# Layer 2's ternary 3x3 convolution in float32r, over the image's upper and lower parts, by half images

## The chip, the cores and the metric

The kernel runs on one core of one Trainium2 chip. Time is the device time of one execution in microseconds (us). Engines are named as the profile names them: PE is TensorE's matmul, PEld its weight load, DVE VectorE, ACT ScalarE, POOL GpSimd.

## The reference, cut to what matters

Four images of 256 channels and 48 x 48 pixels pass four layers, each with a group normalisation before it and a residual sum after it. Layer 2 is a 3x3 convolution with weights of -1, 0 and +1, scaled per output channel:

```python
delta = 0.7 * abs_w.mean(axis=(1, 2, 3), keepdims=True)
ternary = jnp.where(w > delta, 1.0, jnp.where(w < -delta, -1.0, 0.0))
alpha = (abs_w * mask).sum(axis=(1, 2, 3), keepdims=True) / count
...
x = x + conv3x3(_gn(x), alpha * ternary)        # padding 1, NCHW
```

Layer 0 is a 7x7 attention over dilated patches, layer 1 a 3x3 convolution of signs, layer 3 a windowed attention. Layers 0 to 2 go image by image, layer 3 follows for all images.

## The kernel before

An image lies in SBUF as two channel tiles of 128 partitions. Layer 2 normalises it into a padded copy, and each block of 8 output rows (384 columns of PSUM) is the sum of 2 x 9 matmuls:

```python
def conv3x3(pad, w_sb, evacuate):            # layers 1 and 2; the matmul is L457
    for mo in range(NCT):                    # 2 halves of the output channels
        for rb in range(NRB):                # 6 blocks of 8 rows
            ps = ps_cv.tile([P, RB, W], F32, tag="cv", name="cv3")
            n = 0
            for ct in range(NCT):
                for t in range(T1):
                    r0, c0 = rb * RB + t // 3, t % 3
                    nc.tensor.matmul(ps, w_sb[:, ct, t, mo * P : (mo + 1) * P],
                        pad[:, ct, r0 : r0 + RB, c0 : c0 + W],
                        start=(n == 0), stop=(n == NCT * T1 - 1))
                    n += 1
            evacuate(ps, mo, rb)

def layer2(xt, b):
    m, r = gn_stats(xt, ps_st)
    pad = padp.tile([P, NCT, H1, H1], F32, tag="pad", name=f"pad2_{b}")
    clear_border(pad, 1, H1)
    for ct in range(NCT):
        normalise(pad[:, ct, 1 : 1 + H, 1 : 1 + W], xt, ct, m, r)   # one VectorE instruction
    ...                                       # evacuate: xt += alpha * ps, on VectorE
    conv3x3(pad, wl2_sb, evacuate)
    ...                                       # store the image, statistics for layer 3
```

The pool of padded copies has two buffers. One holds the next image's input of layer 0's first convolution (conv0, L334), whose matmuls stand before and after layer 2 in TensorE's order. `prepare_layer2` makes the ternary weights once, beside conv0 of image 0: one load of all weights, absolute values, sums over TensorE, two comparisons. The scheduler decides the order of instructions on each engine.

Of the kernel before, what the change touches and what calls it, by code (L numbers as in the profile page):

```python
# [10 lines left out]
F32 = mybir.dt.float32  # L11
BF16 = mybir.dt.bfloat16
F32R = mybir.dt.float32r
AF = mybir.ActivationFunctionType
ALU = mybir.AluOpType
# [4 lines left out]
P = 128  # L20
B, C, H, W = 4, 256, 48, 48
HW = H * W
NCT = C // P

RB = 8
NRB = H // RB
# [17 lines left out]
T1 = 9  # L44
H1 = H + 2
# [49 lines left out]
def conv_preact_kernel(  # L95
# [22 lines left out]
    nc = tc.nc  # L118
# [51 lines left out]
    def normalise(dst, xt, ct, m, r):  # L170
        nc.vector.tensor_scalar(  # L171
            dst, xt[:, ct], m[:, ct : ct + 1], r[:, ct : ct + 1], ALU.subtract, ALU.mult
        )

    def clear_border(t, pad, n):
        nc.gpsimd.memset(t[:, :, 0:pad, :], 0.0)
        nc.gpsimd.memset(t[:, :, n - pad : n, :], 0.0)
        nc.gpsimd.memset(t[:, :, pad : n - pad, 0:pad], 0.0)
        nc.gpsimd.memset(t[:, :, pad : n - pad, n - pad : n], 0.0)


    with (
# [20 lines left out]
        for ki in range(K0):  # L203
            for ct in range(NCT):
                nc.scalar.dma_start(
                    out=w1_sb[:, ct, ki * K0 : (ki + 1) * K0, :],
                    in_=w1[ct * P : (ct + 1) * P, ki * K0 : (ki + 1) * K0, :],
# [15 lines left out]
        for z in band_d:  # L223
            for f in range(NPH):
                nc.sync.dma_start(
                    out=z[f, 0 : QB * ZROW].rearrange("(p s) -> p s", s=ZROW), in_=zero
# [14 lines left out]
        nc.vector.tensor_add(off, off, bn["be"])  # L241

        wl1_sb = wts.tile([P, NCT, T1, C], BF16, name="wl1_sb")
        wl2_sb = wts.tile([P, NCT, T1, C], F32, name="wl2_sb")
        alpha = wts.tile([P, NCT], F32, name="alpha")

        def prepare_layer1():
# [3 lines left out]

        def prepare_layer2():

            nc.sync.dma_start(out=wl2_sb, in_=wl2.rearrange("(ct p) t o -> p ct t o", p=P))
            tmp = padp.tile([P, 3, T1, C], F32, tag="pad", name="wl2_tmp")
            ab, hi, lo = tmp[:, 0], tmp[:, 1], tmp[:, 2]
            delta = smx.tile([P, 2, C], F32, tag="delta", name="delta", bufs=1)
            ps = ps_st.tile([P, C], F32, tag="st", name="abs_ps")
            for ct in range(NCT):
                nc.scalar.activation(ab, wl2_sb[:, ct], AF.Abs)  # L260
                for t in range(T1):
                    nc.tensor.matmul(
                        ps,
                        ones,
                        ab[:, t, :],
                        start=(ct == 0 and t == 0),
                        stop=(ct == NCT - 1 and t == T1 - 1),
                    )
            nc.vector.tensor_scalar(
                delta[:, 0, :], ps, 1.0 / (C * T1), 0.7, ALU.mult, ALU.mult  # L270
            )
            nc.vector.tensor_scalar_mul(delta[:, 1, :], delta[:, 0, :], -1.0)

            sums = smx.tile([P, NCT, NCT, 2], F32, tag="sums", name="sums", bufs=1)
            for ct in range(NCT):
                nc.scalar.activation(ab, wl2_sb[:, ct], AF.Abs)
                nc.vector.tensor_tensor(
                    hi, wl2_sb[:, ct], delta[:, 0:1, :].to_broadcast([P, T1, C]), ALU.is_gt
                )
                nc.vector.tensor_tensor(  # L280
                    lo, wl2_sb[:, ct], delta[:, 1:2, :].to_broadcast([P, T1, C]), ALU.is_lt
                )
                nc.vector.tensor_sub(wl2_sb[:, ct], hi, lo)
                nc.vector.tensor_add(hi, hi, lo)
                nc.vector.tensor_mul(ab, ab, hi)
                for what, src in ((0, ab), (1, hi)):
                    for mo in range(NCT):
                        ps = ps_st.tile([P, 1], F32, tag="st", name="sum_ps")
                        for t in range(T1):
                            nc.tensor.matmul(  # L290
                                ps,
                                src[:, t, mo * P : (mo + 1) * P],
                                ones[:, 0:1],
                                start=(t == 0),
                                stop=(t == T1 - 1),
                            )
                        nc.vector.tensor_copy(sums[:, ct, mo, what : what + 1], ps)
            nc.vector.tensor_add(sums[:, 0], sums[:, 0], sums[:, 1])
            nc.vector.tensor_scalar_max(sums[:, 0, :, 1], sums[:, 0, :, 1], 1.0)
            nc.vector.reciprocal(sums[:, 1, :, 1], sums[:, 0, :, 1])  # L300
            nc.vector.tensor_mul(alpha, sums[:, 0, :, 0], sums[:, 1, :, 1])
# [144 lines left out]
                    xs = by_phase(xt, mo)[:, py, :, k * RP : k * RP + nr, :]  # L446
                    nc.vector.tensor_add(xs, xs, pss[mo][:, py * DIL : (py + 1) * DIL])

        def conv3x3(pad, w_sb, evacuate):
            for mo in range(NCT):  # L450
                for rb in range(NRB):
                    ps = ps_cv.tile([P, RB, W], F32, tag="cv", name="cv3")
                    n = 0
                    for ct in range(NCT):
                        for t in range(T1):
                            r0, c0 = rb * RB + t // 3, t % 3
                            nc.tensor.matmul(  # L457
                                ps,
                                w_sb[:, ct, t, mo * P : (mo + 1) * P],
                                pad[:, ct, r0 : r0 + RB, c0 : c0 + W],  # L460
                                start=(n == 0),
                                stop=(n == NCT * T1 - 1),
                            )
                            n += 1
                    evacuate(ps, mo, rb)

        def layer1(xt, b):
            m, _ = gn_stats(xt, ps_st)
            neg = small.tile([P, NCT], F32, tag="neg", name="neg")
            nc.vector.tensor_scalar_mul(neg, m, -1.0)  # L470
            pad = padp.tile([P, NCT, H1, H1], BF16, tag="pad", name=f"pad1_{b}")
            clear_border(pad, 1, H1)

            for ct in range(NCT):
                nc.scalar.activation(
                    pad[:, ct, 1 : 1 + H, 1 : 1 + W], xt[:, ct], AF.Sign, bias=neg[:, ct : ct + 1]
                )

            def evacuate(ps, mo, rb):
                xs = xt[:, mo, rb * RB : (rb + 1) * RB, :]  # L480
                nc.vector.tensor_add(xs, ps, xs)

            conv3x3(pad, wl1_sb, evacuate)

        def layer2(xt, b):
            m, r = gn_stats(xt, ps_st)
            pad = padp.tile([P, NCT, H1, H1], F32, tag="pad", name=f"pad2_{b}")
            clear_border(pad, 1, H1)
            for ct in range(NCT):
                normalise(pad[:, ct, 1 : 1 + H, 1 : 1 + W], xt, ct, m, r)  # L490

            def evacuate(ps, mo, rb):
                xs = xt[:, mo, rb * RB : (rb + 1) * RB, :]
                nc.vector.scalar_tensor_tensor(  # L494
                    xs, ps, alpha[:, mo : mo + 1], xs, ALU.mult, ALU.add
                )

            conv3x3(pad, wl2_sb, evacuate)
            for ct in range(NCT):
                nc.sync.dma_start(out=x3_d[b][ct * P : (ct + 1) * P], in_=xt[:, ct])  # L500
            m, r = gn_stats(xt, ps_st)
            nc.vector.tensor_copy(st3[:, b, 0, :], m)
            nc.vector.tensor_copy(st3[:, b, 1, :], r)
# [20 lines left out]
        for b in range(B + 1):  # L524
            last = b - 1
            if b == B:
                attend0(last, NBLK - 1)
                finish0(last, NBLK - 2)
                finish0(last, NBLK - 1)
                layer1(xts[last], last)  # L530
                layer2(xts[last], last)
                break
# [462 lines left out]
```

## Time and profile before

| | before |
|---|---|
| time, median (range) | 5846.0 us (5844.4 to 5849.5, 4 runs) |
| span of the profiled run | 5851.2 us |
| TensorE busy | 95% of the span |
| layer-2 convolution on TensorE (float32) | 560.2 us in 4 images: 139.5 us in image 0, 141.7 in the last |
| layer-1 convolution (bfloat16, half as many records) | 147.6 us |
| granted TensorE clock, mean | 0.982 |

In a line of a group, the columns are: line of the kernel, engine, operation, output <- inputs, shape, count | total busy us, mean ns of one | idle time just before and what ended it. A timeline line has start and duration in us first. The lines that carry the reading stand in the prediction.

### The profile page before, as it was taken

The page shows a single profiled execution, that of the slowest core. Times are in us where ns is not written, and L with a number is a line of the kernel's source. Part 1 is how long each engine was busy: PE and PEld are TensorE (multiplying, and loading weights), DVE is VectorE, ACT ScalarE, POOL GpSimd, SP SyncE. Part 2 cuts the span into 40 slices and gives each one's busy share as a digit, 9 for nine tenths or more (in the row PEclk, how much of TensorE's full clock was granted, in tenths as well). Part 3 has the DMA queues.
Part 4 walks back from the last instruction along what each step waited for, and adds up shares of the span by engine and source line. Part 5 has one row for each costly group of instructions (what it writes and reads, how often), then busy time and mean ns, then how long its engine had stood idle before and what let it go on. Part 6 is the DMA issues. An engine that isn't in the chain of part 4 may idle for free.

```text
span 5851.2 us, 65381 instructions
## 1 busy us (share of the span) xinstructions
PE 5535.8 (95%) x25684; PEld 2763.7 (47%) x25684; DVE 2169.4 (37%) x5202; ACT 1075.7 (18%) x2179; POOL 732.0 (13%) x1193
## 2 busy tenths in 40 slices
PE   7999999999999999978999999999999999899997
PEld 3555555555555555544444444444444444444443
DVE  1210101110110110214566555565645665566654
ACT  0000000010000000013322223322223222233221
POOL 0000000000000000034202213112223012100111
PEclk9999999999999999889999999999999999999998
DMA  3000000000000001035122242132342222411322
GB/s 124 6 11 10 7 13 25 11 11 5 33 11 5 11 17 12 12 113 158 60 66 81 78 123 82 42 95 81 86 117 70 65 81 77 116 30 44 91 58 64
DMA packets 234350, 321.67 MB, mean 55 GB/s; under 512 B 94107, under 2 KB 199355, under 8 KB 227259
## 3 DMA queue, kind: packets, MB, share of 16 engines
q1 hardware_dynamic: 191995, 201.45, 12.9%
q0 software_dynamic: 38160, 108.02, 6.9%
q10 hardware_dynamic: 3888, 8.00, 0.4%
q8 instruction: 205, 3.36, 0.2%
q14 instruction: 102, 0.84, 0.0%
HBM read 209.43 MB, written 109.46 MB: 54 GB/s over the span
## 4 chain that ended last, share of the span: by engine, by line
PE 82%; DVE 6%; issue 4%; DMA 4%; POOL 3%; ACT 1%; SPq 0%; DVEq 0%; POOLq 0%; ACTq 0%
PE cv L334 27%; PE acc L817 25%; PE cv L457 12%; PE s L765 11%; DVE sm L807 4%; PE out_ps L879 3%; PE proj_ps L635 2%; PE ap L437 1%; DVE o L874 1%; POOL xn L621 1%; DMA nr<-n_d 1%; PE proj_ps L674 1%; DMA o_d<-stage 0%; POOL sq L683 0%; ACT sm L815 0%
## 5 line engine op out<-in xcount | busy, mean ns | idle before, releaser
L807 DVE TENSOR_TENSOR sm<-s,masks 128x240 f32<-128x240 f32 (+22 forms) x4032 | 1689.0, 456 | 1120.6 <-PE s L765 687.9
L817 PE MATMUL acc<-sm,vst 128*64 128x320 f32 (+14 forms) x13440 | 1985.9, 398 | 120.7 <-DVE sm L807 104.3
L334 PE MATMUL cv<-pad,w_sb 128*128 128x480 f32 (+1 forms) x3920 | 1575.4, 560 | 0.2 <-DVE pad L313 0.2
L817 PEld LDWEIGHTS acc<-sm,vst 128*64 128x64 f32 x13440 | 762.0, 136 | 851.6 <-issue 405.1
L334 PEld LDWEIGHTS cv<-pad,w_sb 128*128 128x128 f32 x3920 | 735.4, 189 | 785.8 <-issue 726.1
L815 ACT COPY sm<-s 128x528 f32<-128x528 f32 (+3 forms) x1440 | 690.7, 486 | 1601.9 <-DVE sm L807 1587.8
L765 PE MATMUL s<-qs,kst 128*128 128x320 f32 (+3 forms) x2880 | 838.6, 374 | 9.6 <-DVE sm L807 8.6
L765 PEld LDWEIGHTS s<-qs,kst 128*128 128x128 f32 x2880 | 436.1, 189 | 742.7 <-issue 694.8
L457 PE MATMUL cv<-pad,wl_sb 128*128 128x384 f32 (+1 forms) x2592 | 707.8, 436 | 4.6 <-DVE pad L171 3.2
L358 DVE TENSOR_TENSOR e<-lg,bn_inv 120x196 f32<-120x196 f32 (+1 forms) x20 | 7.2, 361 | 1171.9 <-PE lg L355 1171.9
L457 PEld LDWEIGHTS cv<-pad,wl_sb 128*128 128x128 f32 x1728 | 327.6, 190 | 233.7 <-issue 5.0
L343 ACT ACTIVATE k<-cv,b_sb 128x480 f32<-128x480 f32 (+1 forms) x20 | 12.9, 644 | 1606.5 <-PE cv L334 1606.5
L879 PE MATMUL out_ps<-o,wout_sb 128*128 128x384 f32 x576 | 222.5, 514 | 45.3 <-DVE o L874 44.4
L831 POOL DMA_DIRECT2D o_d<-stage x192 | 96.9, 505 | 1312.0 <-ACT sm L815 1055.9
L827 ACT COPY stage<-acc 128x384 f32<-128x384 f32 x288 | 137.8, 479 | 484.5 <-PE acc L817 479.6
L387 POOL COPY flat<-pad 128x240 f32<-128x240 f32 (+1 forms) x80 | 34.6, 460 | 1516.8 <-PE trx L400 1480.8
L494 DVE SCALAR_TENSOR_TENSOR x<-cv,alpha,x 128x384 f32<-128x384 f32 x48 | 29.7, 618 | 501.9 <-PE cv L457 501.9
L879 PEld LDWEIGHTS out_ps<-o,wout_sb 128*128 128x128 f32 x576 | 100.2, 191 | 139.5 <-DVE o L874 66.9
L437 PEld LDWEIGHTS ap<-seen,xT 120*128 120x128 f32 (+2 forms) x832 | 110.7, 212 | 16.1 <-ACT seen L430 10.1
L139 ACT ACTIVATE rsq_s<-gn_v 128x2 f32<-128x2 f32 x16 | 3.3, 204 | 622.2 <-DVE gn_v L166 622.1
L674 PE MATMUL proj_ps<-wv_sb,xn 128*128 128x256 f32 x288 | 96.6, 441 | 20.2 <-ACT sg L652 12.6
L457 PEld LDWEIGHTS <-wl_sb 128*128 128x128 bf16 x864 | 85.6, 99 | 62.6 <-issue 6.5
(118 smaller groups left out, 1978.3 us busy)
## 6 DMA issues: line engine op xcount, KB each, us to landing
qs<-q_d SPq DMA_DIRECT2D x384, 96.0 KB, 2.2
kst<-k_d SPq DMA_DIRECT2D x128, 288.0 KB, 7.6
o_d<-stage POOLq DMA_DIRECT2D x192, 144.0 KB, 2.3
o<-o_d POOLq DMA_DIRECT2D x24, 1152.0 KB, 5.7
rc<-r_d POOLq DMA_DIRECT2D x192, 144.0 KB, 3.5
q_d<-hl SPq DMA_DIRECT2D x48, 384.0 KB, 2.8
k_d<-hl SPq DMA_DIRECT2D x48, 384.0 KB, 2.5
v_d<-vt SPq DMA_DIRECT2D x24, 768.0 KB, 3.3
```

The source lines that it names most:

```text
L334: nc.tensor.matmul(ps, w1_sb[:, ct, t, :], pad[:, ct, :, r0 : r0 + nr, c0 : c0 + HP], start=(n == 0), stop=(n == NCT * T0 - 1),)
L437: nc.tensor.matmul(pf[:, f, a:e], xTs[k + i][:n, f, mo * P : (mo + 1) * P], seen[:n, 1 + i, a:e], start=(i == 0), stop=(i == near[-1]),)
L457: nc.tensor.matmul(ps, w_sb[:, ct, t, mo * P : (mo + 1) * P], pad[:, ct, r0 : r0 + RB, c0 : c0 + W], start=(n == 0), stop=(n == NCT * T1 - 1),
L635: nc.tensor.matmul(ps, proj[name][:, ct, mo * P : (mo + 1) * P], xn[:, ct], start=(ct == 0), stop=(ct == NCT - 1),)
L674: nc.tensor.matmul(ps, xn[:, ct, c, :], proj["v"][:, ct, :], start=(ct == 0), stop=(ct == NCT - 1),)
L765: nc.tensor.matmul(s[:, j, 0 : (r1 - r0) * (c1 - c0)], kst[2 * pr + j][:, a * NKC + c, :], qs[:, j, r0:r1, c0:c1], start=True, stop=True,)
L807: nc.vector.tensor_mul(dst, src, mask[wi][:, mr : mr + n, mc : mc + p1 - p0] .unsqueeze(1) .to_broadcast([P, 2, n, p1 - p0]),)
L815: nc.scalar.copy(dst, src)
L817: nc.tensor.matmul(accs[wi][64 * j : 64 * (j + 1)].rearrange("p (r w) -> p r w", w=W)[:, r0:r1, c0:c1], vst[pr][:, a * NKC + c, j, :], sm[ ...
L827: nc.scalar.copy(stage[:, wi, :], accs[wi])
L831: nc.gpsimd.dma_start(out=o_d[b][rb, h * D : (h + 1) * D, :], in_=stage[64 * j : 64 * j + D].rearrange("p w n -> p (w n)"),)
L879: nc.tensor.matmul(ps, wout_sb[:, kt, mo * P : (mo + 1) * P], t["o"][:, kt % NCT, kt // NCT, :], start=(kt == 0), stop=(kt == NW * NCT - 1),)
```

## The change

The image is split into an upper part (what float32r keeps of it) and the rest; the change takes it that both are exact in float32r, as are -1, 0 and +1, so that two float32r matmuls give what one float32 matmul gave. Each result is only checked against a tolerance. Two parts of a whole padded image do not fit in SBUF beside the rest, so the layer goes by halves of 24 rows; and the float32r weights leave no room for raw ones, so these are loaded piecewise, three times half of them. The core of the diff:

```diff
-        wl2_sb = wts.tile([P, NCT, T1, C], F32, name="wl2_sb")
+        wl2_sb = wts.tile([P, NCT, T1, C], F32R, name="wl2_sb")
 ... prepare_layer2: load_raw(0), load_raw(1), later load_raw(0) again, into one scratch tile
-        def conv3x3(pad, w_sb, evacuate):
+        def conv3x3(parts, w_sb, evacuate, first, rbs):
 ...
+                            for pad in parts:
                                 nc.tensor.matmul(
 ... layer2:
-            for ct in range(NCT):
-                normalise(pad[:, ct, 1 : 1 + H, 1 : 1 + W], xt, ct, m, r)
+            for half in range(2):
+                pad = padp.tile([P, 2, NCT, HR + 2, H1], F32R, tag="pad", name=f"pad2_{b}")
 ... six border memsets on GpSimd
+                pieces = [(0, 13), (13, HR + 1)] if half == 0 else [(HR - 1, HR), (HR, 36), (36, H)]
+                for ct in range(NCT):
+                    for y0, y1 in pieces:
+                        t = bandp.tile([P, 13, W], F32, tag="l2t", name="l2t", bufs=1)
+                        nc.vector.tensor_scalar(t, ..., ALU.subtract, ALU.mult)
+                        nc.scalar.copy(hi, t)
+                        nc.gpsimd.tensor_sub(pad[:, 1, ct, ...], t, hi.bitcast(F32))
+                conv3x3([pad[:, 0], pad[:, 1]], wl2_sb, evacuate, half * HR, ...)
```

In the changed kernel conv0 is L340, layer 0's apply matmuls (L437 before) are L443, the 3x3 convolution L466, the normalisation of a piece L526, the upper part L536, the lower part L537, and the border memsets L516 to L518.

More of the change, by code (lines that the diff above doesn't have):

```diff
@@ L252, in prepare_layer2, with load_raw @@
         def prepare_layer2():
-            nc.sync.dma_start(out=wl2_sb, in_=wl2.rearrange("(ct p) t o -> p ct t o", p=P))
             tmp = padp.tile([P, 3, T1, C], F32, tag="pad", name="wl2_tmp")
-            ab, hi, lo = tmp[:, 0], tmp[:, 1], tmp[:, 2]
+            raw, u, v = tmp[:, 0], tmp[:, 1], tmp[:, 2]
+            def load_raw(ct):
+                nc.sync.dma_start(out=raw, in_=wl2[ct * P : (ct + 1) * P])
             delta = smx.tile([P, 2, C], F32, tag="delta", name="delta", bufs=1)
@@ L259, in prepare_layer2 @@
             for ct in range(NCT):
-                nc.scalar.activation(ab, wl2_sb[:, ct], AF.Abs)
+                load_raw(ct)
+                nc.scalar.activation(u, raw, AF.Abs)
                 for t in range(T1):
@@ L264, in prepare_layer2 @@
                         ones,
-                        ab[:, t, :],
+                        u[:, t, :],
                         start=(ct == 0 and t == 0),
@@ L274, in prepare_layer2 @@
             sums = smx.tile([P, NCT, NCT, 2], F32, tag="sums", name="sums", bufs=1)
-            for ct in range(NCT):
-                nc.scalar.activation(ab, wl2_sb[:, ct], AF.Abs)
+            for ct in reversed(range(NCT)):
+                if ct < NCT - 1:
+                    load_raw(ct)
                 nc.vector.tensor_tensor(
-                    hi, wl2_sb[:, ct], delta[:, 0:1, :].to_broadcast([P, T1, C]), ALU.is_gt
+                    u, raw, delta[:, 0:1, :].to_broadcast([P, T1, C]), ALU.is_gt
                 )
                 nc.vector.tensor_tensor(
-                    lo, wl2_sb[:, ct], delta[:, 1:2, :].to_broadcast([P, T1, C]), ALU.is_lt
+                    v, raw, delta[:, 1:2, :].to_broadcast([P, T1, C]), ALU.is_lt
                 )
-                nc.vector.tensor_sub(wl2_sb[:, ct], hi, lo)
-                nc.vector.tensor_add(hi, hi, lo)
-                nc.vector.tensor_mul(ab, ab, hi)
-                for what, src in ((0, ab), (1, hi)):
+                nc.vector.tensor_sub(wl2_sb[:, ct], u, v)
+                nc.vector.tensor_add(u, u, v)
+                nc.scalar.activation(v, raw, AF.Abs)
+                nc.vector.tensor_mul(v, v, u)
+                for what, src in ((0, v), (1, u)):
                     for mo in range(NCT):
@@ L447, in apply0 @@
                     nc.vector.tensor_add(xs, xs, pss[mo][:, py * DIL : (py + 1) * DIL])
-        def conv3x3(pad, w_sb, evacuate):
+        def conv3x3(parts, w_sb, evacuate, first, rbs):
             for mo in range(NCT):
-                for rb in range(NRB):
+                for rb in rbs:
                     ps = ps_cv.tile([P, RB, W], F32, tag="cv", name="cv3")
@@ L455, in conv3x3 @@
                         for t in range(T1):
-                            r0, c0 = rb * RB + t // 3, t % 3
-                            nc.tensor.matmul(
-                                ps,
-                                w_sb[:, ct, t, mo * P : (mo + 1) * P],
-                                pad[:, ct, r0 : r0 + RB, c0 : c0 + W],
-                                start=(n == 0),
-                                stop=(n == NCT * T1 - 1),
-                            )
-                            n += 1
+                            r0, c0 = rb * RB + t // 3 - first, t % 3
+                            for pad in parts:
+                                nc.tensor.matmul(
+                                    ps,
+                                    w_sb[:, ct, t, mo * P : (mo + 1) * P],
+                                    pad[:, ct, r0 : r0 + RB, c0 : c0 + W],
+                                    start=(n == 0),
+                                    stop=(n == len(parts) * NCT * T1 - 1),
+                                )
+                                n += 1
                     evacuate(ps, mo, rb)
@@ L481, in evacuate @@
                 nc.vector.tensor_add(xs, ps, xs)
-            conv3x3(pad, wl1_sb, evacuate)
+            conv3x3([pad], wl1_sb, evacuate, 0, range(NRB))
         def layer2(xt, b):
             m, r = gn_stats(xt, ps_st)
-            pad = padp.tile([P, NCT, H1, H1], F32, tag="pad", name=f"pad2_{b}")
-            clear_border(pad, 1, H1)
-            for ct in range(NCT):
-                normalise(pad[:, ct, 1 : 1 + H, 1 : 1 + W], xt, ct, m, r)
             def evacuate(ps, mo, rb):
@@ L496, in evacuate @@
                 )
-            conv3x3(pad, wl2_sb, evacuate)
+            HR = H // 2
+            keep = bandp.tile([P, NCT, 1, W], F32, tag="keep", name="keep", bufs=1)
+            nc.gpsimd.tensor_copy(keep, xt[:, :, HR - 1 : HR, :])
+            for half in range(2):
+                pad = padp.tile([P, 2, NCT, HR + 2, H1], F32R, tag="pad", name=f"pad2_{b}")
+                at = 1 - half
+                i0, i1 = half * (HR - 1), H - (1 - half) * (HR - 1)
+                n = i1 - i0
+                zr = half * (HR + 1)
+                for s in range(2):
+                    nc.gpsimd.memset(pad[:, s, :, zr : zr + 1, :].bitcast(F32), 0.0)
+                    nc.gpsimd.memset(pad[:, s, :, at : at + n, 0:1].bitcast(F32), 0.0)
+                    nc.gpsimd.memset(pad[:, s, :, at : at + n, H1 - 1 : H1].bitcast(F32), 0.0)
+                pieces = [(0, 13), (13, HR + 1)] if half == 0 else [(HR - 1, HR), (HR, 36), (36, H)]
+                for ct in range(NCT):
+                    for y0, y1 in pieces:
+                        kept = half == 1 and y0 == HR - 1
+                        t = bandp.tile([P, 13, W], F32, tag="l2t", name="l2t", bufs=1)
+                        t = t[:, 0 : y1 - y0]
+                        nc.vector.tensor_scalar(
+                            t,
+                            keep[:, ct] if kept else xt[:, ct, y0:y1],
+                            m[:, ct : ct + 1],
+                            r[:, ct : ct + 1],
+                            ALU.subtract,
+                            ALU.mult,
+                        )
+                        ty = at + y0 - i0
+                        hi = pad[:, 0, ct, ty : ty + y1 - y0, 1 : 1 + W]
+                        nc.scalar.copy(hi, t)
+                        nc.gpsimd.tensor_sub(
+                            pad[:, 1, ct, ty : ty + y1 - y0, 1 : 1 + W], t, hi.bitcast(F32)
+                        )
+                conv3x3(
+                    [pad[:, 0], pad[:, 1]],
+                    wl2_sb,
+                    evacuate,
+                    half * HR,
+                    range(half * NRB // 2, (half + 1) * NRB // 2),
+                )
             for ct in range(NCT):
```

## The prediction

> **What bounds the kernel now.** I read the page first, the chain of waits on it, the groups of instructions by shape, and then TensorE's own timeline around one convolution of layer 2.
>
> ```profile
> PE 5535.8 (95%) x25684; PEld 2763.7 (47%) x25684; DVE 2169.4 (37%) x5202; ACT 1075.7 (18%) x2179; POOL 732.0 (13%) x1193
> ...
> PE 82%; DVE 6%; issue 4%; DMA 4%; POOL 3%; ACT 1%; SPq 0%; DVEq 0%; POOLq 0%; ACTq 0%
> PE cv L334 27%; PE acc L817 25%; PE cv L457 12%; PE s L765 11%; DVE sm L807 4%; PE out_ps L879 3%; PE proj_ps L635 2%; PE ap L437 1%; DVE o L874 1%; POOL xn L621 1%; DMA nr<-n_d 1%; PE proj_ps L674 1%; DMA o_d<-stage 0%; POOL sq L683 0%; ACT sm L815 0%
> ```
>
> TensorE is busy 95% of the span and carries 82% of the chain that ends last. L457 is the 3x3 convolution of layers 1 and 2 together: 12% of the span. The groups by shape split it.
>
> ```profile
> L457 PE MATMUL cv<-pad,wl_sb 128*128 128x384 f32 x1728 | 560.2, 487 | 3.2 <-DVE pad L171 3.2
> L457 PE MATMUL cv<-pad,wl_sb 128*128 128x384 bf16 x864 | 147.6, 334 | 1.4 <-ACT pad L475 1.4
> L457 PEld LDWEIGHTS cv<-pad,wl_sb 128*128 128x128 f32 x1728 | 327.6, 190 | 233.7 <-issue 5.0
> ```
>
> Both layers have 4 images x 2 output halves x 6 row blocks x 18 taps = 864 matmuls. In bfloat16 (layer 1) they are 864 records; in float32 (layer 2) 1728, two per matmul. Layer 2 holds TensorE for 560.2 us and waits only 3.2 us in all four images, so any time off these matmuls comes off the span. The timeline gives the pace (start, duration, line):
>
> ```profile
> 803.31 139.52 PE L457 MATMUL cv<-pad,wl_sb 128*128 128x384 f32 x432
> ...
> 1898.56 35.78 PE L457 MATMUL cv<-pad,wl_sb 128*128 128x384 bf16 x216
> ...
> 2410.32 141.66 PE L457 MATMUL cv<-pad,wl_sb 128*128 128x384 f32 x432 [3.16 <-DVE pad L171]
> ```
>
> One float32 matmul costs 139.52 / 216 = 0.646 us, four times the 35.78 / 216 = 0.166 us of a bfloat16 one: four passes over 384 columns against one. The third line is the last image, the only one with nothing beside it, where the normalisation shows (3.16 us).
>
> What a float32r matmul costs is seen only in layer 3, whose scores use it, always in pairs:
>
> ```profile
> 2901.30 0.44 PE L765 MATMUL s<-qs,kst 128*128 128x384 f32 x1
> ...
> 2901.30 0.62 PE L765 MATMUL s<-qs,kst 128*128 128x384 f32 x2
> ```
>
> Narrowing the window to the first of a pair gives an end at 0.44 us; the pair ends at 0.62. So the second, with its own weight load, adds 0.175 us (durations 442 and 339 ns, span 0.615). Pairs of 320 columns add about 0.148. The 64 columns between them cost 27 ns, 0.42 ns each: one pass, one record. If float32r needed two passes it would be 53 ns.
>
> **What the Trainium skill says.** "TensorE: Matmul & The Clock Gate", section "Wait — 56ns, not 53.3ns?", gives N / 2.4 GHz + 2.5 ns between warm matmuls: 162.5 ns for 384 columns. The trace agrees for bfloat16: (35.78 us less the 0.33 us that one record lasts) / 216 = 164 ns at granted clock 1.00; the other three images took 36.86 to 37.57 us at 0.97 to 0.95. "FP8 and Floating Point Precision", section "TensorE Precision Notes", says true FP32 makes 4 passes through the array; the 0.646 us agree. "TensorE: Matmul & The Clock Gate", section "LDWEIGHTS (loading the stationary operand)", gives columns / 1.2: 107 ns for 128, less than a 160 ns pass, so hidden. The trace agrees: the float32 matmuls of 120 columns at L437 (24 records in 2.80 us, where two passes are 100 ns) pace at 117 ns, a floor set by the load and below 160. "GPSIMD Engine Reference", section 3.1, has a two-input float32 op at 4497 ns for 2048 elements, 2.2 ns each; the trace has one point, the same kind of subtraction into float32r:
>
> ```profile
> L654 POOL TENSOR_TENSOR hl<-sg,hl 128x384 fp32r<-128x384 f32 x96 | 95.7, 1000 | 5.4
> L815 ACT COPY sm<-s 128x528 f32<-128x528 f32 x384 | 236.0, 615 | 434.3 <-DVE sm L807 430.2 <-DVE rsq_u L142 4.1
> ```
>
> **The change, part by part.**
>
> *Matmuls.* Each of the 864 becomes two float32r matmuls (upper and lower part, same weights), each one record and one pass: 1728 records as before, of half the time. Per image 432 x p. At p = 164 ns (bfloat16 at full clock) 70.9 us; at 175 ns (the scores pair, which may hold a start-up) 75.6 us. The denser stream may lose clock as bfloat16's did in three of four images; I take p = 168 ns: 72.6 us. Four images: 290 instead of 560, a saving of 270 us.
>
> *Preparation.* Before, a tile is normalised by two VectorE instructions of 1558 ns into a whole padded image. Now a half image is 4 or 6 pieces, each VectorE normalise -> ScalarE copy (upper) -> GpSimd subtract (lower), through one scratch buffer, so pieces run one after another. Estimates for a piece of 576 to 624 elements: VectorE 0.52 (1558 ns scaled from 2304 elements, plus a fixed part), ScalarE 0.68 (615 ns for the 528 columns above), GpSimd 1.45 to 1.55 (1000 ns at 384 plus 2.2 ns per further element): about 2.8 us per piece. None of these engines is a bound; what counts is how long TensorE waits.
>
> *Start of half 0, images 0 to 2.* The order of the built program keeps layer 2's statistics behind the 98 conv0 matmuls, as before (second group-mean matmul at 796.25 us, scale ready at 800.63), and places transposes and apply matmuls (L437) of layer 0 between. Upper part of piece 1 is ready about 2.5 us after the scale (ScalarE first does two other copies), its lower part at 4.1, second channel tile at 8.2 and 9.8. The order interleaves two PSUM banks, so 18 matmuls (3.0 us) stand between each. Followed through, TensorE waits 0.5 + 1.0 + 0.9 = 2.4 us, against 0 before.
>
> *Between the halves.* The other pad buffer holds the next image's conv0 input, so half 1 uses half 0's buffer and cannot be written before its last matmul. From there: six border memsets on GpSimd (1.5 us), the kept row, then the chain: upper part at 3.2 us, lower at 4.7, second channel tile at 9.4 and 10.9. The scheduler has put about 3.5 us of layer 0's work (transposes, apply) into this gap, and 22 conv matmuls (3.7 us) run before the second channel tile. Waits: 0.4 + 0.7 + 1.0 + 1.0 = 3 us per image. The filler is moved, not added.
>
> *Last image.* Nothing fills half 0's start: 11.5 us until the stream is free, with 40 matmuls (6.8 us) in it: 4.7 us of waiting against 1.7 from scale to matmul before, so +3. Its half 1 gets a free buffer (in the built order its memsets stand before half 0's subtractions), so no gap.
>
> *Weights.* The ternary weights are made from tiles loaded three times (1.15 MB each) instead of once. All of it stands beside conv0 of image 0; the third load is wanted some 20 us after it can be issued, and loads of this size land in 8 us. Cost 0 to 2 us.
>
> Sum: -270 + 3 x 5.4 + 3 + 1 = -250; 5845 - 250 = 5595 us. PSUM evacuation (618 ns per block on VectorE against 6.0 us of matmuls per block) stays hidden.
>
> **The rivals.**
>
> 1. *Two parts give back what float32r gains.* If float32r in a long stream paces like a float32 record (323 ns), because the pair of passes or an unhidden 189 ns weight load sets it, nothing is saved: 5865 us. Against it: the 0.42 ns per column of the scores, and L437's 117 ns pace with a load each. A middle form, loads hidden only partly and p near 200 ns, would give 5650. For it: no long float32r stream exists in this trace.
>
> 2. *The half-image hand-over becomes the wait.* If GpSimd is slower (VectorE's normalise and GpSimd share access to the memory; two flat copies took 1.86 us beside the normalise against 0.72 alone), each piece may take 4 us, and the six pieces after half 0's last matmul would stall 10 us more per image: 5625 us. Against: VectorE waits for GpSimd on the one scratch buffer, so they rarely overlap.
>
> 3. *The clock gives way.* Float32 ran at 1.00, bfloat16 at 0.95 to 0.97 in three of four images. If float32r falls to 0.90, 290 becomes about 313: 5620 us. If the clock holds at 1.00 and p is 164, 5587.
>
> **Range and chances.** Middle 5595. Faster end: p = 162 ns and no hand-over waits, 560 - 280 = -280, 5565; I use 5570. Slower end: p = 175 ns (+12) and 7 us more waiting per image (+28): 5635. Leaving 2% (5728 us) would need p above about 245 ns with the waits as estimated. Faster by over 2%: 0.96; within 2%: 0.03; slower: 0.01.
>
> **What would show it.** In the changed kernel's groups, the line of the 3x3 convolution should hold 1728 float32r records, and half 0 and half 1 of an image should each run 216 records in about 36 us on the timeline, with weight loads of about 189 ns hidden. Between them, TensorE should have two or three idle stretches of about 1 us released by ScalarE's copy or GpSimd's subtraction. Layer 3, from its first projection on, should have the same length. The prediction is wrong if the 216 records take over 45 us, if idle time before the convolution exceeds 10 us per image, or if conv0 of image 0 shows a wait for the weight load.

## The result, and the profile after

The changed kernel takes 5622.6 us (median of 4 runs, 5620.7 to 5631.1) against 5846.0, a ratio of 0.962 (95% interval 0.9603 to 0.9636). A ratio is the mean time of one kernel's runs over that of the other's of the same rounds, so it is not quite the ratio of the medians. The predicted 5595 was 28 us too low, inside the range of 5570 to 5635.

The page of the changed kernel, busy time and chain of waits:

```profile
PE 5289.7 (94%) x25684; PEld 2747.3 (49%) x25684; DVE 2176.7 (39%) x5234; ACT 1100.8 (20%) x2219; POOL 780.0 (14%) x1269
...
PE cv L340 28%; PE acc L865 26%; PE s L813 11%; PE cv L466 8%; DVE sm L855 4%; PE out_ps L927 3%; PE proj_ps L683 2%; PE ap L443 1%; DVE o L922 1%; POOL xn L669 1%; DMA nr<-n_d 1%; DMA o_d<-stage 1%; PE proj_ps L722 1%; POOL sq L731 1%; POOL pad L537 0%
```

The number of matmul records is exactly the same, 25684, and TensorE has 246 us less to do. The 3x3 convolution falls from 12% of the chain to 8%; no other engine takes its place. The groups by shape:

```profile
L466 PE MATMUL cv<-pad,wl_sb 128*128 128x384 f32 x1728 | 323.4, 347 | 11.8 <-ACT pad L536 7.0 <-POOL pad L537 4.5
L466 PEld LDWEIGHTS cv<-pad,wl_sb 128*128 128x128 f32 x1728 | 315.2, 190 | 17.3 <-POOL pad L537 8.2 <-ACT pad L536 5.9 <-issue 3.1
```

The profile prints float32r as f32. 1728 records as predicted, in 323.4 instead of 560.2 us, with 11.8 us of idle time before them instead of 3.2, released by the upper and the lower part. TensorE's timeline of image 0 shows one half and the beginning of the next:

```profile
802.85 0.43 PE L466 MATMUL cv<-pad,wl_sb 128*128 128x384 f32 x1
803.12 0.82 PE L443 MATMUL ap<-seen,xT 120*128 120x75 f32 x6
804.14 3.52 PE L466 MATMUL cv<-pad,wl_sb 128*128 128x384 f32 x18 [0.20 <-POOL pad L537]
808.26 1.00 PE L466 MATMUL cv<-pad,wl_sb 128*128 128x384 f32 x4 [0.60 <-ACT pad L536]
809.74 35.34 PE L466 MATMUL cv<-pad,wl_sb 128*128 128x384 f32 x193 [0.48 <-POOL pad L537]
...
853.85 0.82 PE L466 MATMUL cv<-pad,wl_sb 128*128 128x384 f32 x3 [0.72 <-ACT pad L536]
855.24 34.79 PE L466 MATMUL cv<-pad,wl_sb 128*128 128x384 f32 x190 [0.57 <-POOL pad L537]
```

The long stretches give the pace: (34.79 - 0.34) / 189 and (35.34 - 0.34) / 192 are 182.3 ns a matmul; a stretch without breaks, measured by itself below, gives 181.4. I had taken 168. The short idle stretches in brackets are where I had put them.

The pace also shows in the busy time by stretch (columns: stretch, length, then busy us and count of PE, PEld, DVE, ACT, POOL, granted clock, DMA share, GB/s). One such stretch of the changed kernel:

```profile
809.90:844.90 35.00, 35.00 (x193) 35.00 (x194) 6.60 (x12) 0.68 (x1) 1.33 (x1) 1.00 0.00 1
```

and one of the kernel before:

```profile
803.30:942.80 139.50, 139.50 (x435) 81.86 (x434) 13.81 (x24) 0.00 (x0) 0.00 (x0) 1.00 0.02 9
```

At the same clock of 1.00, weight loads are now in flight during 35.00 of 35.00 us, where before they covered 81.86 of 139.50. This invites the reading that the weight load sets the new pace. The experiments test it, and it falls.

### The profile page after: what moved, and what is told of

Read it like the earlier page. It is cut to its first block, busy times and chain, and to the rows that moved or that the text cites. A ratio compares the mean times of both kernels' runs of the same rounds, so it can differ in the third digit from the quotient of the medians.

```text
span 5619.8 us, 65529 instructions
## 1 busy us (share of the span) xinstructions
PE 5289.7 (94%) x25684; PEld 2747.3 (49%) x25684; DVE 2176.7 (39%) x5234; ACT 1100.8 (20%) x2219; POOL 780.0 (14%) x1269
## 4 chain that ended last, share of the span: by engine, by line
PE 81%; DVE 6%; issue 4%; DMA 4%; POOL 3%; ACT 1%; SPq 0%; DVEq 0%; POOLq 0%; ACTq 0%
PE cv L340 28%; PE acc L865 26%; PE s L813 11%; PE cv L466 8%; DVE sm L855 4%; PE out_ps L927 3%; PE proj_ps L683 2%; PE ap L443 1%; DVE o L922 1%; POOL xn L669 1%; DMA nr<-n_d 1%; DMA o_d<-stage 1%; PE proj_ps L722 1%; POOL sq L731 1%; POOL pad L537 0%
## 5 line engine op out<-in xcount | busy, mean ns | idle before, releaser
L340 PE MATMUL cv<-pad,w_sb 128*128 128x480 f32 (+1 forms) x3920 | 1577.0, 560 | 0.2 <-DVE pad L319 0.2
L340 PEld LDWEIGHTS cv<-pad,w_sb 128*128 128x128 f32 x3920 | 735.2, 189 | 785.6 <-issue 727.5
L466 PE MATMUL cv<-pad,wl_sb 128*128 128x384 f32 (+1 forms) x2592 | 471.0, 343 | 13.2 <-ACT pad L536 7.0
L466 PEld LDWEIGHTS cv<-pad,wl_sb 128*128 128x128 f32 x1728 | 315.2, 190 | 17.3 <-POOL pad L537 8.2
L443 PEld LDWEIGHTS ap<-seen,xT 120*128 120x128 f32 (+2 forms) x832 | 110.5, 209 | 16.7 <-ACT seen L436 11.5
L466 PEld LDWEIGHTS <-wl_sb 128*128 128x128 bf16 x864 | 85.6, 99 | 62.6 <-issue 6.3
L443 PE MATMUL ap<-seen,xT 120*128 120x120 f32 (+3 forms) x832 | 113.5, 294 | 1.8 <-ACT seen L436 1.5
```

Of the source, the lines that this page charges most:

```text
L340: nc.tensor.matmul(ps, w1_sb[:, ct, t, :], pad[:, ct, :, r0 : r0 + nr, c0 : c0 + HP], start=(n == 0), stop=(n == NCT * T0 - 1),)
L443: nc.tensor.matmul(pf[:, f, a:e], xTs[k + i][:n, f, mo * P : (mo + 1) * P], seen[:n, 1 + i, a:e], start=(i == 0), stop=(i == near[-1]),)
L466: nc.tensor.matmul(ps, w_sb[:, ct, t, mo * P : (mo + 1) * P], pad[:, ct, r0 : r0 + RB, c0 : c0 + W], start=(n == 0), stop=(n == len(parts) ...
```

## The experiments

Theory: what is missing from the predicted gain is the pace of a float32r matmul, 181 ns instead of 168 (1728 x 13 ns = 23 us), and the rest of the sum is about right. Rivals: the missing time is in the waits between the halves; or in the weight preparation; or in a lower clock. Below that stands a second question: why 181 ns.

### pace: what a matmul of each type and size costs

The kernel's body is replaced by streams of 216 matmuls, each stream into one PSUM bank, with nothing else running (the result is wrong):

```diff
+    stream("r384", "f32r", 8, 48)      # type, rows, columns of a 50-wide padded tile
+    stream("r480", "f32r", 10, 48)
+    ...                                # 288, 192, 96 columns; one weight tile; 64 weight columns
+    stream("r384flat", "f32r", 8, 48, contiguous=True)
+    stream("b384", "bf16", 8, 48)      # and the same in bfloat16 and float32
```

> No result of the reference (wrong on purpose): 17 streams of 216 TensorE matmuls each, one after another, all into one PSUM bank per stream, float32r, bfloat16 and float32, moving 96 to 480 columns. In the changed kernel a float32r matmul of 384 columns took 181 ns where I had predicted 168. Theory 1, the weight load sets it: float32r pace is the larger of the stream (N / 2.4 ns) and a load of about 181 ns, so 96, 192, 288 and 384 columns all pace near 181 ns, 480 columns at about 203, and weights of 64 columns bring 384 down to about 163. Theory 2, a fixed cost beside the stream: N / 2.4 + 21 ns at every N: 61, 101, 141, 181, 221 ns. Theory 3, the four-byte stream itself is slower: 0.472 ns a column, 45, 91, 136, 181, 227 ns, and 64-column weights change nothing. bfloat16 should show 163 to 166 ns at 384 and float32 323, as in the kernel before. Always the same weights: unchanged, unless the hardware leaves the load out.

TensorE's timeline inside the float32r streams of 480, 384, 288 and 192 columns, then 64-column weights, then bfloat16 with 384 (the name prints without its size; pace = (duration - one record) / (count - 1)):

```profile
202.69 43.48 PE L151 MATMUL r<-mv_f32r,w_f32r 128*128 128x480 f32 x193
...
162.82 35.36 PE L151 MATMUL r<-mv_f32r,w_f32r 128*128 128x384 f32 x194
...
251.71 18.59 PE L151 MATMUL r<-mv_f32r,w_f32r 128*128 128x288 f32 x133
...
289.73 10.44 PE L151 MATMUL r<-mv_f32r,w_f32r 128*128 128x192 f32 x92
...
387.73 34.55 PE L151 MATMUL r384half<-mv_f32r,w_f32r 128*64 128x384 f32 x191
...
507.74 32.47 PE L151 MATMUL b<-mv_bf,w_bf 128*128 128x384 bf16 x196
```

| moving columns | float32r ns | above N / 2.4 | bfloat16 ns | float32 ns per record (two passes) |
|---|---|---|---|---|
| 480 | 224.4 | 24.4 | 205.3 | 402.6 |
| 384 | 181.4 | 21.4 | 164.8 | 322.6 |
| 288 | 138.5 | 18.5 | - | - |
| 192 | 111.7 | 31.7 | 83.7 | 162.6 |
| 96 | 213.3, at clock 0.50 | - | 44.4 | 111.7 |

Theory 1, the weight load as the bound, is refuted: the pace keeps falling below 181 ns with fewer columns, and half the weight columns take 180.0 ns, though their load records last 134 ns and fill 75% of the time instead of all of it. A floor exists, but at 111.7 ns, the same for float32r of 192 columns and float32 of 96; that the load sets it is likely, but no stream of 192 columns with narrower weights was run. The load of 128 four-byte columns is a record of 187 to 192 ns beside every float32 or float32r stream at full clock, paced at anything from 111.7 to 402.6 ns; where the pace is shorter the records overlap, and the PEld row is full without being a bound. Neither of the others holds alone: the excess is 18.5 to 24.4 ns, neither constant nor proportional. Always the same weights cost 181.5 ns once the clock was back at 1.00, so repeating them saves nothing. The pace of 181 ns belongs to a float32r stream of this layout, without pieces, halves or a throttled clock. One stream of the edit is missing from the table: 384 columns in one piece of memory took 175.7 ns (37.96 us between two starts, over 216).

### pace_rows: where the 21 ns lie

The same streams of 384 columns, laid out in rows of different length and alignment (wrong):

```diff
+    stream("conv", "f32r", 8, 48, 50)              # rows, columns, row stride in words
+    stream("aligned", "f32r", 8, 48, 64, shift=1)  # shift: starts move by 0 to 2 words, 1: never
+    stream("unaligned", "f32r", 8, 48, 64)
+    ...                                            # long rows, one row, short rows; bfloat16 too
```

> No result of the reference (wrong on purpose): 13 streams of 216 matmuls, nearly all of 384 moving columns, which differ in how these columns lie in memory. In the first pace run float32r took 224.4, 181.4 and 138.5 ns for 10, 8 and 6 rows of 48 columns (24.4, 21.4 and 18.5 ns above N / 2.4), 175.8 ns for 384 columns in one piece, and bfloat16 164.8 ns for the same rows of 48. Theory A, a cost per row of the moving operand of 1.5 ns beside a fixed 9.5 ns: 2 long rows of 192 take 172 to 173 ns, 24 short rows of 16 take 205 ns, starts on aligned addresses change nothing. Theory B, a slower stream per column whatever the rows (0.447 ns a column): all at 176 to 182 ns. Theory C, addresses that are not aligned (rows of 50 words, taps shifted by one word): aligned rows fall to about 165 ns, the shifted ones stay at 181. Narrow weights (32 columns): 180 ns as with 64. The last two, 96 columns, repeat a surprise of the first run: float32r fell to a granted clock of 0.50 at this size, 213 ns a matmul, bfloat16 stayed at 1.00 and 44 ns; the same is expected here if the size causes it.

The timeline; a pace is the distance between two starts over 216:

```profile
54.17 39.42 PE L148 MATMUL conv<-mv_f32r,w_f32r 128*128 128x384 f32 x216
93.43 38.32 PE L148 MATMUL aligned<-mv_f32r,w_f32r 128*128 128x384 f32 x216
131.59 39.53 PE L148 MATMUL unaligned<-mv_f32r,w_f32r 128*128 128x384 f32 x216
170.95 38.72 PE L148 MATMUL longrows<-mv_f32r,w_f32r 128*128 128x384 f32 x216
209.51 38.56 PE L148 MATMUL onerow<-mv_f32r,w_f32r 128*128 128x384 f32 x216
247.91 37.61 PE L148 MATMUL onerowaligned<-mv_f32r,w_f32r 128*128 128x384 f32 x216
285.36 44.08 PE L148 MATMUL shortrows<-mv_f32r,w_f32r 128*128 128x384 f32 x216
329.27 36.72 PE L148 MATMUL bshortrows<-mv_bf,w_bf 128*128 128x384 bf16 x216
```

This gives 181.8 ns for the convolution's layout, 176.7 with aligned rows, 178.5 for two long rows, 177.8 for one row at shifting starts, 173.4 for one aligned row, and 203.3 for 24 short rows. bfloat16 takes 169.3 ns for the short rows and 162.2 for one row. So each of my theories has a piece and none the whole: 4 to 6 ns are the unaligned starts, 3 to 4 ns the eight rows (0.6 ns a row; 24 rows cost 25 ns more than one, about 1.1 ns a row, so it is not one price per row; bfloat16 pays 0.3), and 13 ns above N / 2.4 remain for one aligned row, not explained by these runs. Theory A's number for long rows, 172 to 173 ns, was missed by 6 ns. Narrow weights of 32 columns took 182.8 ns, so the load is again not it. The 96-column float32r stream fell to clock 0.50 again.

### bf16_halves: the same kernel with the other type

```diff
-        wl2_sb = wts.tile([P, NCT, T1, C], F32R, name="wl2_sb")
+        wl2_sb = wts.tile([P, NCT, T1, C], BF16, name="wl2_sb")
-                pad = padp.tile([P, 2, NCT, HR + 2, H1], F32R, ...)
+                pad = padp.tile([P, 2, NCT, HR + 2, H1], BF16, ...)
```

> The changed kernel with both parts and the ternary weights in bfloat16 instead of float32r, all else alike (16 bits of the image instead of 24, less exact on purpose). Same number of matmuls, same pieces, same hand-over. Theory (the extra 15 to 20 ns of a float32r matmul belong to float32r, by its weight load or its stream): pace 164 to 170 ns, 1728 x 0.0155 = 27 us less: about 5595 us, my predicted time. Rival (the pace of 181 ns comes from the two-part order, the clock or the accumulation of 36 matmuls): unchanged, 5622 us.

It took 5594.7 us (5593.1 to 5603.6, 4 runs; ratio 0.957), the theory's number. Its long stretch of 190 matmuls in image 0 took 31.49 us, (31.49 - 0.33) / 189 = 164.9 ns each; 1728 x (181.4 - 164.9) = 28.5 us, and 5622.6 - 5594.7 = 28. The fit is closer than its parts: idle time before the layer-2 matmuls grew by 3.8 us here (from 11.8 to 15.6). The two-part order and the 36-deep accumulation are thus not what costs the 17 ns. The result stays within the tolerance, with 16 bits of the image instead of 24.

### upper_only: one part instead of two

```diff
-                for s in range(2):                  # border memsets, of both parts before
+                for s in range(1):
-                        nc.gpsimd.tensor_sub(pad[:, 1, ct, ...], t, hi.bitcast(F32))
-                    [pad[:, 0], pad[:, 1]],
+                    [pad[:, 0]],
```

> The changed kernel with the upper part alone: no subtraction on GpSimd, 864 float32r matmuls instead of 1728 (less exact on purpose[...]). Theory: TensorE's stream is what counts, so 864 x 0.1825 us = 158 us and a few us of waits go: about 5460 us. Rival: the preparation of the pieces, which now has half as much matmul work beside it, becomes the wait: 5480 us or more, with idle time of TensorE before the convolution above 15 us in all.

It took 5450.6 us (5449.4 to 5451.9, 4 runs; ratio 0.932). 864 x 181.4 ns = 157 us explain most of the 172; the idle time before the float32r matmuls fell from 11.8 to 3.0 us:

```profile
L466 PE MATMUL cv<-pad,wl_sb 128*128 128x384 f32 x864 | 160.9, 348 | 3.0 <-ACT pad L536 3.0
```

The rival falls: without the subtraction, preparation is no longer a wait in images 0 to 2, although there is half the matmul work to hide it. Pieces of 576 or 624 elements now follow each other in 1.3 to 1.4 us (normalisations at 801.11, 802.42 and 803.81 us in image 0) instead of 2.7, so the lower part's link of the chain, on GpSimd, is half of a piece. About 6 us of the gain I have not attributed. This version, without the lower part, passes the check against the reference too: the check cannot tell whether the second matmul is needed.

### piece_major: the waits made smaller

The second group of runs began with the unedited changed kernel as a yardstick.

> The changed kernel once more, unedited, as the yardstick of this group: 5621 to 5624 us, ratio 0.962.

It took 5623.7 us (5615.1 to 5631.6, 4 runs; ratio 0.962). The edit:

```diff
-                for ct in range(NCT):
-                    for y0, y1 in pieces:
+                for y0, y1 in pieces:
+                    for ct in range(NCT):
```

> The changed kernel with the two loops of the preparation exchanged: the first piece of both channel tiles before the second piece of either. The results are bit for bit the same. The second channel tile of the first row block is ready one piece (2.7 us) earlier. Theory (the waits of the chain of pieces are on the path): idle time of TensorE before the layer-2 convolution falls from 11.8 us to about 5 us, and the time by about 6 us, to about 5616 us. Rival: the scheduler's order of matmuls changes with it, and the waits only move to the next row block: unchanged.

It took 5603.6 us (5601.3 to 5613.4, 5 runs; ratio 0.959, interval 0.9577 to 0.9603, against 0.9608 to 0.9635 for the yardstick), about 17 us less in the mean than the yardstick of the same rounds, and faster than the two kernels before and after, with the arithmetic of the latter. The group's line:

```profile
L466 PE MATMUL cv<-pad,wl_sb 128*128 128x384 f32 x1728 | 319.3, 346 | 5.6 <-ACT pad L536 3.1 <-POOL pad L537 2.5
```

The idle time fell as expected, from 11.8 to 5.6 us, but the gain is larger than that. In the timeline of image 0, the first half now runs from 803.69 to 844.27 us, with one break, instead of 802.85 to 845.08 with three: 1.65 us less, where the idle time named there fell by 1.08 (0.60 + 0.48). The second half gained 1.77 us, of which 0.2 is layer 0's work that moved out of it; its named idle time fell by 0.91. A break costs more than its bracket, because the records of matmuls overlap (one lasts 343 ns, the next begins 181 ns later), and the end of the last one before a break covers part of it. From the first attention matmul of image 0's layer 0 to the first projection of layer 3, the profiled runs of yardstick and edit differ by 2141.3 - 2132.5 = 8.8 us. Before that stretch they differ by 2.3 us and in layer 3 by 1.5, which makes the 12.6 us between the two profiled spans; the rest of the 17 us lies in the spread between runs, 12 to 17 us in either kernel. I claim only the 8.8 for the edit.

### thrice_loaded: the weight preparation alone

The kernel before, with the changed `prepare_layer2` and nothing else:

```diff
-            nc.sync.dma_start(out=wl2_sb, in_=wl2.rearrange("(ct p) t o -> p ct t o", p=P))
+            def load_raw(ct):
+                nc.sync.dma_start(out=raw, in_=wl2[ct * P : (ct + 1) * P])
 ... as in the changed kernel, but wl2_sb stays F32
```

> The kernel before with only the new preparation of the ternary weights (three loads of half the weights through one scratch tile instead of one load of all; everything else float32 and whole images as before). In the changed kernel conv0's second and third block, which this preparation stands beside, took 118.6 us from one attention matmul to the next instead of 113.7. Theory: the preparation costs this, by the granted clock (0.88 against 0.93) and not by a wait: +5 us, about 5851 us, and the same interval of 118 to 120 us. Rival (my prediction's step): 0 to 2 us, at most 5848 us, and an interval of about 114 us; the 5 us then come from something else in the changed kernel.

It took 5850.0 us (5846.6 to 5858.2, 5 runs), ratio 1.001 with an interval of 0.9997 to 1.0022; by time alone that is no difference. The stretch between the first two attention matmuls is clear. First the kernel before, then this one:

```profile
204.20:317.90 113.70, 113.70 (x387) 66.24 (x385) 30.98 (x33) 8.68 (x6) 2.60 (x4) 0.92 0.06 7
```

```profile
202.20:320.80 118.60, 118.60 (x386) 70.27 (x385) 31.66 (x33) 8.68 (x6) 2.59 (x4) 0.88 0.08 17
```

The interval grew by 4.9 us, exactly as in the changed kernel (118.6), although TensorE has the same work and stays busy throughout in all three. The profiled runs of the changed kernel and of its six repeats and variants all show it, 118.6 to 120.3 us. The granted clock is 0.88 instead of 0.92. In both kernels some of the blocks of one-column sums (18 records each) take 3.84 us instead of 2.06, at a granted clock of 0.50 instead of 1.00: two of eight before with one more partly slowed, three of eight here with two more partly slowed. So the third load made nothing wait; the new order of small matmuls among conv0's goes with a lower clock. Which of the two, the order or the moment, sets the clock was not separated.

### bf16_whole and upper_whole: without halves

In bfloat16 both parts of a whole image fit in one buffer, and the upper part alone fits in float32r:

```diff
-            for half in range(2):
-                pad = padp.tile([P, 2, NCT, HR + 2, H1], BF16, ...)
+            pad = padp.tile([P, 2, NCT, H1, H1], BF16, ...)     # bf16_whole, pieces of 12 rows
+            pad = padp.tile([P, NCT, H1, H1], F32R, ...)        # upper_whole, no pieces
```

> As bf16_halves, but as a whole image in one pad buffer (two bfloat16 parts of a whole image are no larger than two float32r parts of half an image), in pieces of 12 rows, both channel tiles alternating. It takes away the hand-over between the halves. Theory: the hand-over costs 1.5 us of idle TensorE in images 0 to 2, so 5 us less than bf16_halves: about 5590 us. Rival: the hand-over costs more than its idle time shows (10 us or more in all, by work moved into the gap): 5580 us or less.

> The upper part alone, in float32r, normalised by VectorE straight into one whole padded image as in the kernel before (less exact on purpose; no halves, no pieces, no subtraction). Against upper_only (5450.6 us), which had 3.0 us of idle time before the convolution. Theory: the hand-over between the halves costs what its idle time shows and a little for the moved work: 5442 to 5447 us. Rival: halves cost nothing once there is no subtraction: 5450 us.

bf16_whole took 5576.8 us (5575.4 to 5579.2, 4 runs; ratio 0.953): 18 us less than bf16_halves, not 5. Idle time of TensorE before the convolutions of layers 1 and 2 fell from 17.0 to 5.2 us (1.4 of each is layer 1); with bfloat16's faster matmuls the same chain of pieces leaves larger gaps (15.6 us) than float32r's 11.8, and, as in piece_major, gaps cost more than they show. bf16_whole also takes the tiles alternately, so its 18 us are halves and piece order together. The rival's 5580 us or less is thus met, but not its cause: in piece_major the order alone gained about as much. It is the fastest version here with two parts, at 16 bits of the image.

upper_whole took 5456.1 us (5455.2 to 5458.8, 4 runs; ratio 0.934), some 5 us more than upper_only, whose ratio of 0.932 comes from other rounds on another chip; the intervals of the two ratios overlap (0.9323 to 0.9348 and 0.9305 to 0.9333). The theory's gain of 3 to 9 us is missed, and the rival stands within the noise: without the subtraction, halves are no loss. Per image the layer-2 stretch got 1.4 us shorter without them, but the next stretch of conv0 took 70.4 instead of 67.8 us, since transposes and apply matmuls that upper_only had in the gap between its halves now stand there. A gap with other work put into it costs nothing.

## Why the prediction was right, and where it was off

The prediction held: faster by over 2%, time inside the range. Step by step, with the profiled runs (5851.2 and 5619.8 us, 231.4 us apart):

| step | predicted us | measured us |
|---|---|---|
| matmuls, 1728 records | -270 | -244 |
| waits for the pieces and between the halves, images 0 to 2 | +16 | +16 |
| waits in the last image | +3 | +1 |
| weight preparation | +1 | +5 |
| start, layer 0 and layer 3 | 0 | -9 |

The first row is 3 x 432 x (322.9 - 181.4) ns = 183 us and 60.5 us for the last image (141.7 us before, 81.2 now without its one break). The waits are these 183 us less what images 0 to 2 really gained from one layer-2 stretch and the conv0 stretch after it: 55.2, 56.2 and 56.1 us; in the yardstick's trace they come to 17.6 us. In the last image, from the second group-mean matmul to the end of the convolution, 59.3 us were gained (145.2 before, 85.9 now), 1.2 less than the 60.5. The last row is what remains: 2.5 us before the first attention matmul, 2.2 in layer 3, and the rest in stretches of layer 0 that move by up to 4 us from run to run.

That the time lay inside the range is partly luck. The range was built on paces of 162 to 175 ns, and 181.4 lies outside; what covered it was the slow end's allowance of 28 us for further waits, which were not needed, and the 9 us of the last row, which no step had foreseen.

- **The kernel is bound by TensorE, so time off these matmuls comes off the span.** Right: upper_only took off another half of the records and 172 us.
- **One record and one pass.** Right, 181 ns and not 323.
- **p = 168 ns.** This term was mis-sized: 181.4 ns. I had one measurement of float32r, 175 ns from the scores pairs, and treated part of it as a start-up that a long stream would hide. A long stream hides nothing of it: pace gives 181.4 at this layout, bfloat16 164.8. Nor was the pair wrong: its moving operand is 384 columns in one piece, and long streams of one piece took 173.4 to 177.8 ns. What I left out is that the convolution's operand, eight rows at unaligned starts, is slower than the layout I had measured. The 13 ns make 23 us, and the halves of image 0 took 42.2 and 42.3 us on the timeline, with the breaks and some work of layer 0 in them, instead of about 36. (The 164 ns that I had for bfloat16 is 164.9: 216 records have 215 distances.)
- **The clock may give way (rival 3).** It did not in images 0 to 2, where it stayed at 1.00. The last image shows 0.96, but the kernel before loses nearly as much there; the table below the list shows it, and it leaves rival 3 less than 1 us.
- **The weight load is hidden because 107 ns are less than a pass.** Right as to the bound (floor 111.7 ns, half-width weights no faster), though the PEld row at 100% suggested otherwise; that the floor is the load's was not tested by itself.
- **A piece takes 2.8 us, through one scratch buffer.** Right: in image 0's second half, successive normalisations stand at 846.11 and 848.83 us, 2.72 apart. Rival 2 fell; GpSimd needed 1.32 us for 576 elements and 1.41 for 624, below my estimate of 1.45 to 1.55, VectorE 0.58, a little above it. The 4497 ns for 2048 elements of "GPSIMD Engine Reference", section 3.1, are 2.2 ns each with the fixed part in it; the runs agree, with 2.3 all told, and I had used the figure for each further element, where they show 1.85.
- **Waits of 5.4 us in images 0 to 2.** Right in sum (15.9 us in three images against 16.2), but the brackets show about half of it; I had placed the waits rightly and believed the brackets would carry them.
- **Weights 0 to 2 us, because the load lands in time.** The mechanism I checked (a wait for the third load) did not occur; the 5 us came by the granted clock, which I had not considered there.

The last image by stretches (columns as above):

```profile
2242.10:2250.00 7.90, 7.90 (x30) 7.90 (x31) 1.72 (x3) 2.06 (x3) 3.71 (x3) 0.64 0.01 2
2250.00:2260.00 10.00, 10.00 (x57) 10.00 (x56) 4.05 (x8) 2.50 (x5) 4.36 (x6) 1.00 0.00 0
2260.00:2323.00 63.00, 63.00 (x348) 62.75 (x346) 11.97 (x21) 0.68 (x1) 1.83 (x2) 1.00 0.05 20
```

The stream starts at a clock of 0.64, after some 6 us in which TensorE was mostly idle, and loses 2.8 us by it (81.2 us against 432 x 181.4 ns). The kernel before lost 2.1 us in the same place (141.66 against 139.52 us, clock 0.73 in its first 7.9 us). The slow start probably also gave the pieces time to be ready: after the first matmul there is one break, of 0.74 us, where I had expected several.

## What to carry to other kernels

When an instruction type appears in the trace only in short bursts, take its measured pace as it stands, without a discount for start-up, and only for the layout of the operand that it was measured on; a stream of 200 of them, laid out as the new kernel will lay them out, in a kernel of its own settles it in one run. A weight-load row that is full does not make the load the bound: change the columns it loads, and see whether the pace moves. When pieces feed TensorE through one scratch buffer, order them by what the first accumulation needs, and count a break at more than the idle time printed for it.

## What the Trainium skill lacked or had wrong

- "TensorE: Matmul & The Clock Gate" (section "Wait — 56ns, not 53.3ns?") has one fixed cost of 2.5 ns beside N / 2.4 GHz. bfloat16 kept near it (164.8 ns at 384 columns, 162.2 in one row), float32r did not: 138.5, 181.4 and 224.4 ns at 288, 384 and 480 columns in rows of 48, and 173.4 to 203.3 ns at 384 columns by layout alone. I found no page with a pace for float32r or a cost by rows or alignment of the moving operand.
- The same page, section "LDWEIGHTS (loading the stationary operand)", agrees with the runs if read as a floor on the spacing for four-byte weights: 111.7 ns with 128 columns, against its 107; bfloat16 streams of 96 columns went below it, at 44.4 ns. It does not say that the load's record lasts longer, 187 to 192 ns, and so fills the whole of a float32r stream (35.00 of 35.00 us) without setting its pace.
- The same page, section "What's actually happening", ties the granted clock to how busy TensorE has recently been. Two streams of 96-column float32r matmuls, busy throughout by the profile, ran at clock 0.50 (213 ns each), while float32 of 96 columns ran at 1.00; and some blocks of one-column sums beside conv0 took 3.84 instead of 2.06 us, also at 0.50. Being busy by the profile was not enough here; what sets the two apart was not tested.
